# Linear attention: the gate's logits taken through the values, half of the last softmax in the last round, and the end laid out by hand

## Chip, core and metric

The kernel runs on one core of a Trainium2 chip. The metric is the device time of one execution in microseconds; lower is better. The time before is a median of three executions. The profile and its trace come from one more execution of the same kernel.

## The reference

The model is a small vision transformer of two layers over 128 images, 64 tokens for each and 256 features for each token. The part that the change touches is layer 1: a linear attention over normalised features, and the first lines of the mixture of experts behind it, which need the logits of a gate over the sum.

```python
# layer 1: attention, h is [128 images, 64 tokens, 256]; C = 64, H = 8 heads of 32
q, k, v = heads(ln(h) @ Wq.T + bq), heads(ln(h) @ Wk.T + bk), heads(ln(h) @ Wv.T + bv)
q = softmax(q, axis=-1) * sqrt(d)         # over features
k = softmax(k, axis=-2)                   # over positions
context = einsum('bhnd,bhne->bhde', k, v)
out = einsum('bhnd,bhde->hbne', q, context)
h = h + back_to_tokens(out)
# layer 1: experts
x = ln(h)
logits = x @ gate_w + gate_b              # [8192 tokens, 8 experts]
idx = argmax(softmax(logits))             # each token's expert, then gather, two products, scatter
```

The kernel computes the product of k, q and v in the other order: for each half of a group it forms the 64x64 matrix of `scores` between q and k and mixes the values by it.

## The kernel before

The kernel has stages that follow one another: tokenizer, attention with relu, an attention of experts, and then `linear_attention`, `route` and `experts`. Only `linear_attention`, the tables in `Routing` and the first lines of `route` are touched. An image is a partition (128 of them), and h lies in memory as `hd`, `[image, token, feature]`.

`linear_attention` treats the 64 tokens as 16 groups of four (`Group`) and the 256 features as 4 pairs of head halves (`Heads`, n from 0 to 3). A group is loaded (L1131), its statistics are taken on DVE (`statistics`, L1139 and L1140), `factors` on POOL makes the inverse root, `normal` on ACT normalises (L1150), and `transpose` brings it into feature order in `xT` by eight transposes on PE (L1159) and two copies on ACT (L1160).

The work stands in four rounds of 16 steps, one round for each n, in an order written out by hand (`manual_schedule`; an engine's instructions run in that order). Each step i of round n makes the query and key product of one token (`queries_keys`, L1182, four passes of 512 columns), then `prepare` does a piece of a later group: statistics of group g+3, normalisation of group g+1, and at the last of every four steps the transposes of group g+1 and the load of group g+5. Then come the steps listed in `work` for (n, i), then the bias add that takes the product out of PSUM on DVE (`queries_keys_kept`, L1186), and in eight of the steps two tokens' value products (`values`, L1196) with a copy on ACT (L1199). Products of both kinds share three PSUM buffers.

The list `work` is filled by `at(round, step, function)`. For head n it holds, in round n+1:

- `values_transposed` (L1209, eight groups of four transposes, with bias by ACT at L1212).
- `largest`, `maximum`, `spread`, `q_less`: the maximum of q over features, by DVE and two small PE products.
- `k_max` (L1249, DVE), `k_less` (L1253, POOL), `k_exp` and `q_exp` (L1257 and L1243, ACT), `k_sum` (L1260, DVE), `k_over_sum` (L1266, POOL).
- `scores` (L1275, 128 passes, two halves alternating), `scores_kept` and `scores_sums` (`am`, L1281 to L1288).
- `mixed` (L1297, four steps of 32 passes), `added` (L1305, DVE, into h) and `written` (two stores of 2 MB, L1309). h itself is loaded at step 8 of the head's own round (L1174).

In round n+2 the new h of head n is brought into feature order by 32 transposes (`transposed`, L1319, copies on ACT at L1323), multiplied by the gate's weights (`gates`, L1332) and added to `lgs` (L1342 and L1344), and `moments` takes 64 statistics for the later norm (L1313). After the last round there are no more queries, and the rest of heads 2 and 3 runs as rounds 4 and 5 without them. This is the tail. `route` (from L1518) then joins the statistics, turns `lgs` back by eight transposes (L1533), and subtracts the mean's part (L1539).

Of the kernel before, what the change touches and what calls it, by code (L numbers as in the profile page):

```python
# [14 lines left out]
ALU = mybir.AluOpType  # L15
# [1068 lines left out]
def linear_attention(c, hd, hx, out, lgs, sth, wqk, bqk, wv, bv, wgb):  # L1084
# [4 lines left out]
    tc, nc = c.tc, c.nc  # L1089
    NG = 4  # L1090
    with (
# [17 lines left out]
        wgs = wp.tile([P, 4, 32], F32, name="wgs")  # L1109
        nc.gpsimd.memset(wgs, 0.0)  # L1110
        for j in range(2):
            r = slice(j * 64, j * 64 + 64)
            nc.scalar.dma_start(wgs[r, :, j * E : j * E + E], wgb.rearrange("(p f) e -> f p e", f=64))
        ones = wp.tile([P, P], F32, name="ones")
        nc.gpsimd.memset(ones, 1.0)
# [6 lines left out]
        class Group:  # L1122
# [10 lines left out]
            def statistics(self, j):  # L1133
                if j == 0:
                    self.mv = gp.tile([P, NG, 2], F32, tag="mv", name="mv", bufs=4)
                    self.rs = gp.tile([P, NG], F32, tag="rs", name="rs", bufs=4)
                    self.nb = gp.tile([P, NG], F32, tag="nb", name="nb", bufs=4)
                st = gp.tile([P, 6], F32, tag="st", name="st")
                nc.vector.bn_stats(st, self.x[:, j, :])  # L1139
                nc.vector.bn_aggr(self.mv[:, j, :], st)  # L1140

            def factors(self):
                mean, var = self.mv[:, :, 0], self.mv[:, :, 1]
                nc.gpsimd.tensor_scalar_add(self.rs, var, LN_EPS)
                nc.gpsimd.tensor_tensor(self.rs, self.rs, c.nhalf[:, 0:NG], ALU.pow)
                nc.gpsimd.tensor_mul(self.nb, mean, self.rs)
                nc.gpsimd.tensor_sub(self.nb, c.zero[:, 0:NG], self.nb)

# [13 lines left out]
        class Heads:  # L1162
# [9 lines left out]
            def load(self):  # L1172
                self.h = hp.tile([P, T, 64], F32, tag="h", name="h", bufs=2)
# [30 lines left out]
            def values_transposed(self, k):  # L1204
# [3 lines left out]
                for j in range(4):  # L1208
                    nc.tensor.transpose(pt[:, j, :], self.v[:, 4 * k + j, :], c.ident)  # L1209
                for j in range(4):  # L1210
                    d = 4 * k + j
                    nc.scalar.activation(self.vT[:, d, :], pt[:, j, :], AF.Identity, bias=bvs[:, d : d + 1])  # L1212


            def largest(self, n):
# [5 lines left out]
                else:  # L1221
                    for s in (4, 2, 1):
                        nc.vector.tensor_max(self.m[:, 0:s], self.m[:, 0:s], self.m[:, s : 2 * s])

# [38 lines left out]
            def k_over_sum(self, hh, n):  # L1263
                eng = nc.vector if self.n == 3 and hh == 1 else nc.gpsimd
# [5 lines left out]
            def scores(self):  # L1270
                self.pa = pss.tile([P, 64], F32, tag="ps", name="pa")
                for d in range(32):
                    for hh in range(2):
# [41 lines left out]
            def transposed(self, k):  # L1315
                pt = pst.tile([P, 4, B], F32, tag="pt", name="pt")
                for j in range(4):
                    t = 8 * k + 2 * j
                    nc.tensor.transpose(  # L1319
                        pt[:, j, :], self.h[:, t : t + 2, :].rearrange("p t f -> p (t f)"), c.ident  # L1320
                    )
                hT = hp.tile([P, 4, B], F32, tag=f"hT{k % 4}", name="hT")
                nc.scalar.copy(hT, pt)  # L1323
                if k % 4 == 0:
                    self.hT = []
                self.hT.append(hT)

            def gates(self, x):

                self.pg = pso.tile([P, 4, B], F32, tag="po", name="pg")  # L1330
                for s in range(4):
                    nc.tensor.matmul(  # L1332
                        self.pg[s * 32 : s * 32 + 32].rearrange("p j b -> p (j b)"),
                        wgs[:, self.n, :],
                        self.hT[s].rearrange("p j b -> p (j b)"),
                        start=True,
# [550 lines left out]
```

## Time and profile before

| | us |
|---|---|
| median of 3 executions | 2783.39 (2780.57 to 2786.43) |
| the profiled execution | 2789.24 |
| its span | 2787.4 |
| PE busy | 2610.8 (94% of the span) |
| DVE busy | 2042.3 (73%) |
| ACT busy | 1611.1 (58%) |
| POOL busy | 1629.6 (58%) |

Busy time counts from the start of an instruction to its end. Matmuls are pipelined, so the time between two starts is the better price of one. A 32-bit product is two passes, and each is a row's count in the trace. "PEclk" is the clock that was granted to TensorE, as a share of full speed. An arrow behind a row names what ended the idle time ahead of it.

### The profile page before, as it was taken

The page shows a single profiled execution, that of the slowest core. Times are in us where ns is not written, and L with a number is a line of the kernel's source. Part 1 is how long each engine was busy: PE and PEld are TensorE (multiplying, and loading weights), DVE is VectorE, ACT ScalarE, POOL GpSimd, SP SyncE. Part 2 cuts the span into 40 slices and gives each one's busy share as a digit, 9 for nine tenths or more (in the row PEclk, how much of TensorE's full clock was granted, in tenths as well). Part 3 has the DMA queues.
Part 4 walks back from the last instruction along what each step waited for, and adds up shares of the span by engine and source line. Part 5 has one row for each costly group of instructions (what it writes and reads, how often), then busy time and mean ns, then how long its engine had stood idle before and what let it go on. Part 6 is the DMA issues. An engine that isn't in the chain of part 4 may idle for free. (4 is left out here: it accounts for less than half of the span.)

```text
span 2787.4 us, 76931 instructions
## 1 busy us (share of the span) xinstructions
PE 2610.8 (94%) x33260; PEld 1749.5 (63%) x33260; DVE 2042.3 (73%) x3077; ACT 1611.1 (58%) x3347; POOL 1629.6 (58%) x1389
## 2 busy tenths in 40 slices
PE   7989999999999998899999999998899964999997
PEld 3553444444444443688888888887566644888886
DVE  6759999999998997577777877776566766344443
ACT  3228889888888886466665665665344430233332
POOL 3329888888888897765566655643133211454444
PEclk9999999999999999899999999999899975999999
DMA  3000000000000000000000000000444432555554
GB/s 107 31 12 1 2 1 2 1 2 2 1 2 1 2 2 2 12 11 18 11 18 11 11 18 11 18 10 19 113 96 108 101 83 108 169 191 192 195 194 132
DMA packets 138064, 140.81 MB, mean 51 GB/s; under 512 B 107923, under 2 KB 121509, under 8 KB 130032
## 3 DMA queue, kind: packets, MB, share of 16 engines
q1 hardware_dynamic: 126816, 117.91, 14.1%
q0 software_dynamic: 7648, 14.77, 1.7%
q8 instruction: 263, 4.31, 0.6%
q10 hardware_dynamic: 3248, 3.09, 0.4%
q14 instruction: 89, 0.73, 0.1%
HBM read 103.93 MB, written 32.54 MB: 49 GB/s over the span
## 5 line engine op out<-in xcount | busy, mean ns | idle before, releaser
L495 POOL TENSOR_TENSOR m<-q,k 128x1024 f32<-128x1024 f32 x384 | 719.4, 1906 | 30.6 <-PE sc L297 16.3
L487 DVE TENSOR_TENSOR m<-pc,k 128x2048 f32<-128x2048 f32 (+1 forms) x320 | 646.7, 2058 | 0.5 <-ACT q L431 0.5
L297 PE MATMUL sc<-m,wide 128*32 128x512 f32 x4096 | 529.6, 598 | 12.1 <-DVE m L487 7.2
L496 ACT ACTIVATE m<-m 128x1024 f32<-128x1024 f32 x384 | 402.3, 1049 | 6.0 <-POOL m L495 5.4
L297 PEld LDWEIGHTS sc<-m,wide 128*32 128x32 f32 x4096 | 126.5, 109 | 259.8 <-issue 144.6
L505 ACT ACTIVATE m<-k,q 128x64 f32<-128x64 f32 x1024 | 270.9, 339 | 0.8 <-DVE k L378 0.8
L946 DVE TENSOR_REDUCE mx<-sc 128x16 f32<-128x1024 f32 x128 | 156.1, 1219 | 155.2 <-PE sc L934 125.5
L961 POOL TENSOR_TENSOR e<-e,mx 128x1024 f32<-128x1024 f32 x128 | 243.6, 1903 | 10.1 <-POOL mx L960 0.2
L906 ACT COPY qk<-pqk 128x512 f32<-128x512 f32 x256 | 138.8, 603 | 132.6 <-PE pqk L902 132.6
L960 POOL TENSOR_TENSOR mx<-mx,gate 128x16 f32<-128x16 f32 x128 | 27.8, 217 | 315.5 <-ACT z L991 154.5
L1722 PE MATMUL ph<-xt,w1s 128*128 128x256 f32 x896 | 201.1, 383 | 1.2 <-DVE xt L1713 0.8
L1738 PE MATMUL po<-w2s,hT 128*128 128x256 f32 x896 | 198.0, 379 | 0.0
L973 ACT COPY pT<-pt 128x512 f32<-128x512 f32 x256 | 138.7, 598 | 99.4 <-PE pt L970 98.7
L1722 PEld LDWEIGHTS ph<-xt,w1s 128*128 128x128 f32 x896 | 171.8, 192 | 26.1 <-DVE xt L1713 1.2
L1726 ACT ACTIVATE hT<-ph,w1s 128x256 f32<-128x256 f32 x224 | 93.4, 471 | 155.4 <-PE ph L1722 82.9
L1738 PEld LDWEIGHTS po<-w2s,hT 128*128 128x128 f32 x896 | 168.1, 190 | 21.7
L902 PE MATMUL pqk<-xT,w 64*128 64x128 f32 x2048 | 169.3, 289 | 1.9 <-issue 1.9
L947 DVE TENSOR_TENSOR e<-sc,mx 128x1024 f32<-128x1024 f32 x128 | 156.7, 1224 | 4.4
L1756 POOL DMA_INDIRECT out<-y,rout x56 | 56.8, 1014 | 172.6 <-ACT hT L1726 124.9
L953 DVE TENSOR_REDUCE mx<-e 128x16 f32<-128x1024 f32 x128 | 153.2, 1197 | 2.4 <-ACT e L950 2.4
L902 PEld LDWEIGHTS pqk<-xT,w 64*128 64x128 f32 x2048 | 142.5, 189 | 19.5 <-issue 10.9
L970 PE MATMUL pt<-ident,e 128*128 128x128 f32 x1024 | 142.4, 279 | 4.7 <-POOL e L961 1.2
(289 smaller groups left out, 4985.7 us busy)
## 6 DMA issues: line engine op xcount, KB each, us to landing
w1s<-in_we SPq DMA_DIRECT2D x30, 1028.0 KB
w2s<-in_we SPq DMA_DIRECT2D x30, 1024.0 KB
hd<-h SPq DMA_DIRECT2D x16, 512.0 KB
x<-hd SPq DMA_DIRECT2D x16, 512.0 KB
h<-hd SPq DMA_DIRECT2D x4, 2048.0 KB
hx<-h SPq DMA_DIRECT2D x4, 2048.0 KB
out<-h SPq DMA_DIRECT2D x4, 2048.0 KB
xt<-in_x SPq DMA_DIRECT2D x15, 512.0 KB
```

Source lines behind the costliest of these rows:

```text
L297: nc.tensor.matmul(dst[j : j + 32], wide[:, hf, s : s + 32], part, start=start, stop=stop)
L487: nc.vector.tensor_tensor(m, bcast(self.pq[:, hf, i : i + n], 3, T), k, ALU.max)
L495: nc.gpsimd.tensor_tensor(m, bcast(self.q[:, hf, s : s + 2], 3, T), k, ALU.subtract)
L496: nc.scalar.activation(m, m, AF.Relu)
L505: nc.scalar.activation(self.parts[i, hf][:, q], self.blk.k[:, hf, i], AF.Relu, bias=self.q[:, hf, i - NB // 2, q : q + 1], scale=-1.0,)
L902: nc.tensor.matmul(pq[par][:, k, eh, :], w[r, f : f + P], self.xT[r, fc], start=True, stop=True)
L946: nc.vector.tensor_reduce(mx, sc, AX.X, ALU.max)
L947: nc.vector.tensor_sub(e, sc, bcast(mx, 2, T))
L953: nc.vector.tensor_reduce(self.sm[x], self.e[x], AX.X, ALU.add)
L961: nc.gpsimd.tensor_mul(e, e, bcast(sm, 2, T))
L1722: nc.tensor.matmul(ph[:, j], self.w1[:, w0 : w0 + P], self.xt[:, fc], start=(fc == 0), stop=(fc == 1))
L1738: nc.tensor.matmul(po, self.hT[:, f, r * P : r * P + P], self.w2[:, f, :], start=(f == 0), stop=(f == 7))
```

## The change

The gate's logits are no longer made from the new h. They are a sum of two parts, the one from the h before the attention and the one from the attention's output. The first comes from the normalised groups, through a table `wm` that also holds the gate's own weights: `gates` multiplies `xT` by it in four calls in the head's own round, at steps 1, 5, 9 and 15. Eight of the nine parts of the result go into `u`, a set of values that are already multiplied by the gate; the ninth, times the group's deviation `sd`, is added to `lgs`. `u` is transposed in round n+1 (`gates_transposed`) and mixed by the same `am` as the values (`gates_mixed`), and one addition puts the result into `lgs`, which now lies in token order. The table is made at the start, from three new inputs, by 17 products. `route` takes the difference between the new mean and the group's, which is kept in `mvs`.

In the rounds, `largest` and what follows it stand two steps later, the statistics of `moments` move from steps 8 to 11 to the round's end and the next one's first two steps, the load of h moves into round n+1, and h has a single buffer (for head 3, a buffer of the queries and keys). For head 3, the first half of the softmax stands in steps 9 to 15 of the last round. The end is a written list, `last`, with some of the bias adds on DVE in place of ACT.

```diff
-        wgs = wp.tile([P, 4, 32], F32, name="wgs")
...
+        wm = wp.tile([P, 2, 8, 9, E], F32, name="wm")
+        ub = wp.tile([P, 4, E], F32, name="ub")
+        tmp = hp.tile([P, 32 * P], F32, tag="v", name="tmp")
+        nc.sync.dma_start(tmp[0:32, 0 : 8 * D], wvT)
+        nc.sync.dma_start(tmp[0:32, 8 * D : 8 * D + P], bvT)
+        nc.sync.dma_start(tmp[0:32, 9 * D : 9 * D + 64], wgd)
+        wgd = tmp[0:32, 9 * D : 9 * D + 64]
+        for fc in range(2):
+            pw = pst.tile([P, 8, 8, E], F32, tag="pt", name="pw")
+            for g in range(8):
+                o = g * D + fc * P
+                nc.tensor.matmul(pw[:, g].rearrange("p h e -> p (h e)"), tmp[0:32, o : o + P], wgd, start=True, stop=True)
+            nc.vector.tensor_copy(wm[:, fc, :, 0:8].rearrange("p h e g -> p g h e"), pw)
+            nc.vector.tensor_copy(wm[:, fc, :, 8], bcast(k.wgs[:, fc], 1, 8))
...
+                nc.gpsimd.tensor_mul(self.sd, self.sd, self.rs)
...
-                self.h = hp.tile([P, T, 64], F32, tag="h", name="h", bufs=2)
+                if self.n == 3:
+
+                    h = hp.tile([P, 2, 32, P], F32, tag="qk", name="h3", bufs=2)
...
+                else:
+                    self.h = hp.tile([P, T, 64], F32, tag="h", name="h")
...
+            def gates(self, q):
...
+                pu = pso.tile([P, NG, 9, E], F32, tag="po", name="pu")
+                for j in range(NG):
+                    for fc in range(2):
+                        nc.tensor.matmul(
+                            pu[:, j].rearrange("p o e -> p (o e)"),
+                            g.xT[:, fc, j, :],
+                            wm[:, fc, 2 * self.n + q // 2].rearrange("p o e -> p (o e)"),
...
+                nc.scalar.copy(
+                    self.u.rearrange("p e (t g) -> p e t g", g=8)[:, :, q * NG : q * NG + NG],
...
+                nc.vector.tensor_mul(b, pu[:, :, 8], bcast(g.sd, 2, E))
+                nc.vector.tensor_add(o, o, b)
...
+            def gates_mixed(self):
+                self.pg = pss.tile([P, E, T], F32, tag="ps", name="pg")
+                for e in range(E):
+                    nc.tensor.matmul(self.pg[:, e, :], self.uT[:, e, :], self.am, start=True, stop=True)
...
+            def spread_of(self, hh):
+                pool, tag = (pss, "ps") if hh else (pst, "pt")
+                self.pb = pool.tile([P, 64], F32, tag=tag, name="pb")
+                nc.tensor.matmul(self.pb, ones[0:64], self.dg[0:64, 0:64], start=True, stop=True)
...
-                eng = nc.vector if self.n == 3 and hh == 1 else nc.gpsimd
+                eng = nc.vector if (hh, n) == (1, 0) else nc.gpsimd
...
+            if n > 0:
+                y = heads[n - 1]
+                for i in range(4):
+                    at(n + i // 2, (15, 15, 0, 1)[i], y.moments, 16 * i, 16)
+            at(m, 3, x.load)
             for i in range(4):
-                at(m, 3 + i // 2, x.k_less, i // 2, i % 2)
-                at(m, 4 + i // 2, x.q_less, i)
+                at(m, 2 + i // 2, x.largest, i)
+            at(m, 4, x.maximum)
+            at(m, 4, x.k_max, 0)
...
+            at(m, 5, x.k_max, 1)
...
+                at(m, (5, 6, 6, 7)[i], x.q_less, i)
             for hh in range(2):
-                at(m, 5 + hh, x.k_exp, hh)
-                at(m, 6 + hh, x.q_exp, hh)
...
+                at(m, 6 + hh, x.k_exp, hh)
+                at(m, 7 + hh, x.q_exp, hh)
+                at(m, 7 + hh, x.k_sum, hh)
+                at(m, 8 + hh, x.k_over_sum, hh, 1)
+                at(m, 8 + hh, x.k_over_sum, hh, 0)
...
+            for i in range(2):
+                at(m, 8 + i, x.gates_transposed, i)
...
+            at(m, 12, x.gates_mixed)
+            at(m, 13, x.gates_added)
...
+        at(3, 9, x.largest_of, 0)
+        at(3, 11, x.load)
+        at(3, 11, x.maximum_of, 0)
+        at(3, 12, x.spread_of, 0)
+        for i in range(2):
+            at(3, 11, x.k_less, 0, i)
+            at(3, 12 + i, x.q_less_of, 0, i)
...
+        at(3, 14, x.k_sum, 0)
+        for n, x in enumerate(heads):
+            for q in range(4):
+                at(n, (1, 5, 9, 15)[q], x.gates, q)
+
+        def last():
+            x, y = heads[3], heads[2]
+            x.k_max(1)
+            x.values(0)
...
+            x.largest_of(1)
+            x.values(1)
+            x.values(2)
+            x.k_exp_of(1, 0)
+            x.maximum_of(1)
+            x.values(3)
...
+            x.values(6)
+            y.moments(0, 16)
+            x.scores((0,))
+            x.values(7)
+            y.moments(16, 8)
+            x.scores((1,))
+            x.scores_kept()
+            x.gates_transposed(0)
+            x.scores_sums()
+            x.gates_transposed(1)
+            for k_ in range(8):
+                x.values_transposed(k_)
+            x.gates_mixed()
+            x.mixed(0)
+            x.gates_added()
+            y.moments(24, 8)
+            for k_ in range(4):
+                x.added(k_)
+                if k_ < 3:
+                    x.mixed(k_ + 1)
+                    y.moments(32 + 8 * k_, 8)
+            x.written()
+            y.moments(56, 8)
+            x.moments(0, 64)
...
-        pl = gpp.tile([P, 2, 4, 4, 32], F32, name="pl")
...
+        nc.vector.tensor_sub(mean, mean, k.mvs[:, :, 0])
         nc.vector.tensor_mul(dev, bcast(k.wsum, 1, T), bcast(mean, 2, E))
...
+        nc.vector.tensor_sub(pb, k.lgs.rearrange("p e t -> p t e"), dev)
```

## The prediction, made before the changed kernel was run

> **What bounds the kernel now.** First I read the table of busy time by stage, to see where the change lies and which engine fills it. The columns are length, then busy time of PE, PEld, DVE, ACT and POOL, the granted clock, the DMA share and GB/s.
>
> ```profile
> core 0: us, PE busy (x) PEld busy (x) DVE busy (x) ACT busy (x) POOL busy (x), PEclk, DMA share, GB/s
> 1964.00:2012.00 48.00, 47.76 (x163) 28.88 (x162) 20.57 (x50) 16.94 (x33) 7.42 (x19) 0.95 0.42 90
> 2012.00:2079.00 67.00, 62.47 (x454) 42.30 (x454) 43.95 (x78) 32.74 (x69) 21.55 (x24) 1.00 0.30 64
> 2079.00:2155.00 76.00, 71.59 (x503) 47.72 (x502) 53.43 (x144) 37.38 (x77) 21.55 (x24) 0.98 0.52 122
> 2155.00:2217.00 62.00, 56.36 (x430) 34.19 (x429) 44.43 (x115) 29.72 (x63) 16.63 (x12) 0.97 0.42 88
> 2217.00:2290.00 73.00, 57.43 (x461) 43.69 (x460) 47.71 (x165) 28.88 (x60) 11.25 (x6) 0.81 0.41 101
> ```
>
> Rows one to four are rounds 0 to 3 (16 steps each), row five is the tail up to the routing. The rounds are bound by TensorE, so work added there costs its full length; the tail is a chain across engines at a clock of 0.81. What follows the tail (routing, experts) begins when it ends.
>
> Then the chain that starts the first round, from the timeline:
>
> ```profile
> 1958.86 0.25 POOL L1144 TENSOR_SCALAR rs<-mv 128x4 f32<-128x4 f32 x1 [7.87 <-DVE mv L1140]
> 1960.83 2.07 ACT L1150 ACTIVATE x<-x,nb,rs 128x256 f32<-128x256 f32 x4 [17.06 <-DMA x<-hd]
> 1961.48 2.81 PE L1159 MATMUL pt<-ident,x 128*128 128x128 f32 x8 [5.87 <-ACT x L1150]
> ```
>
> It goes from the last statistics on DVE over POOL and ACT to PE; the first query product stands at 1964.11. Next, the waits of PE from 1964 to 2290 (total, times, longest):
>
> ```profile
> PE pt L1159 <- ACT x L1150: 8.6, 3, 4.0
> PE po L1297 <- DVE am L1288: 5.0, 4, 2.3
> PE pq L1182 <- DVE qk L1186: 1.4, 1, 1.4
> ```
>
> The first is the transposes of x at step 7, behind the exponents on ACT. Last, TensorE rows that price what is new:
>
> ```profile
> 1328.26 1.84 PE L854 MATMUL pg<-wrs,xT 128*128 128x4 f32 x16
> 1329.96 1.07 PE L970 MATMUL pt<-ident,e 128*128 128x128 f32 x8
> ...
> 2061.27 2.00 PE L1297 MATMUL po<-am,vT 64*128 64x64 f32 x32
> 2063.20 1.99 PE L1196 MATMUL pv<-wvs,xT 128*128 128x256 f32 x8
> ...
> 2260.69 12.45 PE L1297 MATMUL po<-am,vT 64*128 64x64 f32 x128 [2.31 <-DVE am L1288]
> 2274.51 3.81 PE L1319 MATMUL pt<-ident,h 128*128 128x128 f32 x16 [1.37 <-DVE h L1305]
> 2253.56 3.95 PE L1275 MATMUL pa<-qk 128*64 128x64 f32 x128
> ```
>
> From start to start: 16 passes with 128-column weights and only 4 moving columns take 1.70 us (0.107 each), a `mixed` step 1.93 at full clock; four of them in the tail take over 12.45, since the clock there is 0.50:
>
> ```profile
> 2265.00:2268.00 3.00, 3.00 (x32) 3.00 (x32) 1.28 (x2) 0.00 (x0) 0.00 (x0) 0.50 0.00 0
> 2268.00:2271.00 3.00, 3.00 (x32) 3.00 (x32) 1.25 (x2) 0.00 (x0) 0.00 (x0) 0.50 0.00 0
> ```
>
> **TensorE work per head.** Removed: 8 groups of 4 transposes at 0.435 and two `gates` at 1.77, 7.0 us; it lay two rounds later, so rounds 2 and 3 had it and the tail had two heads of it. Added: four `gates` of 16 passes with 128-column weights and 72 moving columns. A row with 4 columns gives 0.107 a pass, one with 256 columns 0.216; I take 0.107, as the load of the weights covers 72 columns (64 alone run at 0.060). That is 1.71 a call, 6.9 a head, in the head's own round. Bounds: 0.060 (4 us less a head) and 0.107+0.060=0.167 (4 us more). Besides, 8 transposes of `u` (0.87) and `gates_mixed`, 16 passes at 0.107 (1.71), a round later.
>
> **Start.** New on PE ahead of the transposes: 16 small products, 32 passes with 128-column weights, plus 2 for `ub`. PE is at half clock there (four such passes 0.99 us at 1954.62), and 0.107 doubles to 0.213: 7.2 us from about 1955.9, when `tmp` has landed (issued with the rest at 1949.7, as long in flight as x, 6.6 us, or a little less). The order of DVE puts statistics 2 and 3 of group 0 behind the copies of these products: copies end at about 1963.7, statistics at 1964.4 in place of 1958.7. The chain shifts: **+5.7** (+2, were PE at full clock, to +7).
>
> **Round 0.** 44.8 us of dense PE work and a cold start fill it; four `gates`: **+6.9**.
>
> **Rounds 1 and 2.** The first had 61.7 us of PE work and 5.3 of waits (67.0); the second 68.7 and 7.0 (75.75). PE work becomes 61.7+9.4=71.1 in both. Waits: at step 1 DVE now has the product and sum of `gates` (0.42) ahead of the bias add, so it stands until PE has done `gates` (7.2 us into the round) and is free at 8.2. From there it has `largest` (2.4 and 2.6), `maximum` 0.5, `k_max` 2.2 twice, `q_less` 1.12 four times, `k_sum` 2.56 and in each step statistics 0.55 and bias add 0.6, with no gap. Added up, m is ready at 14.9 (PE stands 1.2 for it), the bias adds of steps 5, 6 and 7 end at 24.3, 27.7 and 32.5. As PSUM holds three products, PE waits 1.3, 0.8 and 1.0 for those. With 1.0 for `am`, as before: 5.3 less what starts earlier, 4.9 in all, so 76.0 each. The wait on ACT goes: of the exponents only one `k_exp` (1.9) now stands ahead of the last normalisation of step 7, and DVE is what is late next. **+9.0** and **+0.2**.
>
> **Round 3.** 53.3 us of work and 9.0 of waits before (62.3). Work +2.9 (9.4 and 0.5 of the half softmax, less 7.0): 56.2. DVE gains the half softmax (2.6+2.2+0.5+2.3+2.6=10.2) and loses half the moments (4.1). Waits: 1.2 for m, 1.5 for the normalisation (POOL's two `k_less` of 1.9, then `k_exp`, end at 24.3), 2.3 ahead of the scores for POOL's three `k_over_sum` (1.9 each, from 30.0), 1.0 for `am`. Then DVE waits at step 12 in `q_less_of` for `pb`, which PE makes only after `mixed(1)` and `gates_mixed`; behind it stand the bias add and `added(1)`, which frees PSUM for `mixed(2)`: 2.3 in all. Sum 64.5: **+2.2**.
>
> **Tail.** Before, 73.0 from 2216.8. After, counted from the end of `gates`: `k_max` and `largest_of` on DVE end at 6.1, PE stands 1.0, seven `values` of 1.72 end at 13.4 with the maximum and exponents of half 1 beside them; scores of one half: the two halves run side by side (0.0305 a pass for both, under the 0.053 that 64 columns need at 512 columns in 0.427), so one alone takes 64 passes at about 0.058, 3.7; `values(7)` 1.7; the other half 3.7: 22.5. Ten groups of transposes, each waiting for a copy (0.65 on DVE, 1.1 on ACT) of the buffer two before: 31.5. `gates_mixed` 1.71, doubled at half clock to 3.4, `mixed` 13.65 (four starts 3.41 apart), 48.6. Last `added` 1.4, `moments` 8 and 64 at 0.13: 59.3. **-13.7**. Half clock is the choice here, as the stretch of transposes before it is like that of 2241 to 2250, which lost the clock. At full clock the end is 51.5 (-21.5); with scores at 1.95 each, 3.5 less.
>
> The trace shows continuous PE work at 0.50 from 2262.4 to 2274, in `mixed` alone. "TensorE: Matmul & The Clock Gate" of the Trainium skill (section "What's actually happening") says that a busy window of about 3.4 us returns the full clock; no window does so in that stretch. By the rule the tail would be about 6 us shorter than by the row; I go by the row.
>
> **Moved DMAs and other things at no cost.** The load of h stands three steps into the next round, on SP behind a load of x, and its single buffer waits for the last head's two writes (4.2 MB at 217 GB/s, 19.3 us). It is issued some 13 us into the round, lands 10 us later and is used at 49; x behind it on SP is fetched four groups ahead. If that cover goes, up to 10 us. The write of head 3 starts at 50 of the tail and needs 19.3; the gather from it comes 55 us after. POOL's extra product (0.2, 16 times) and ACT's copies of `u` (0.41, 16 times, against 32 of 0.54 removed) lie beside PE. Routing: 8 transposes and 8 small subtractions were hidden; a subtraction of 128x512 (0.6) and of 128x64 come: **+0.6**, 0 to 0.9.
>
> **Sum.** 5.7+6.9+9.0+0.2+2.2-13.7+0.6=+10.9. The profiled execution took 2789.24 (span 2787.4), 5.9 above the median of 2783.39; it would become 2800.1, the median **2794.3**.
>
> **Rivals.** *Dense rounds* (the other side): the 16 us of waits of rounds 2 and 3 vanish, since ACT no longer delays step 7 and DVE's lag fits into three PSUM buffers. Rounds 1 to 3 are then 71.5, 71.5 and 57, together -5.0 in place of +11.4: total -5.5, median 2777.9; it turns faster by this much once DVE's bias adds of steps 5 to 7 end 3 us sooner than I count. For it: one wait on ACT was 8.6 of PE's. Against: DVE has no slack from step 1 to 8. *Warm tail*: the clock stays at 1.0: 7.8 less than forecast, +3.1, median 2786.5; against it the two rows at 0.50. *Dear gates*: load and product don't overlap, 0.167 a pass: 16 calls by 0.96, +15.4, median 2810; against it 256-column rows that hide the load. *The half softmax isn't done in time*: its last POOL step ends 0.8 us into the tail and is used at 13.4, so this costs nothing; the built order has every step where it is said to be.
>
> **How the numbers follow.** Forecast 0.53, dense rounds 0.15, warm tail 0.17, dear gates 0.10, others 0.05. About 0.2% (5.6 us) is what a measurement can tell from no change. The forecast's own range, from its bounds, is 2787 to 2802; the full one 2777 to 2808. Slower: nearly all of forecast and dear gates, a third of warm tail: 0.68. Faster: half of dense rounds and half of the others, with a share of 0.05 of warm tail in which waits go too: 0.15. The rest, 0.17, is the same.
>
> **What would show it.** Right: first query product about 5.7 us later; round 0 near 55, rounds 1 and 2 near 76, round 3 near 64, tail near 59 with `mixed` at 0.50 and 3.4 apart; L854's 0.107 in `gates`; PE waiting for DVE's bias add, no longer for ACT's normalisation. Wrong: rounds 1 and 2 near 71, or `mixed` 1.93 apart.

## The result, and the profile after

The changed kernel took 2804.89 us (median of 7, 2798.19 to 2812.98), the kernel before 2786.69 in the same sittings (median of 7, 2780.57 to 2792.56): a ratio of 1.0067, 95% interval 1.0049 to 1.0085. It is slower, as forecast, by 18 us where 11 were forecast; 2804.89 lies above the forecast's own range (2787 to 2802) and inside the full one (to 2808). The kernel before was itself 3.3 slower in these sittings than the 2783.39 that the forecast started from.

The profiled execution took 2804.89 (span 2803.2). A table of stages says where the time went. The stage begins with SP's first issue after the last store of hd; a round runs from its first query product to the next round's, round 3 to the first value product behind it (in the changed kernel behind its last `gates`), and the tail from there to the first instruction of the routing on DVE.

| us | before | after | difference | forecast |
|---|---|---|---|---|
| start, to the first query product | 15.27 | 23.28 | +8.0 | +5.7 |
| round 0 | 47.70 | 53.72 | +6.0 | +6.9 |
| round 1 | 66.96 | 76.98 | +10.0 | +9.0 |
| round 2 | 75.75 | 78.53 | +2.8 | +0.2 |
| round 3 | 62.29 | 71.84 | +9.6 | +2.2 |
| tail | 72.98 | 58.93 | -14.1 | -13.7 |
| routing and experts | 497.61 | 498.54 | +0.9 | +0.6 |
| sum | 838.56 | 861.82 | +23.3 | +10.9 |

The spans differ by 15.8 only, since the untouched stages ahead were 7.5 shorter in the second execution (the stage began at 1941.38 in place of 1948.84). That is chance: in twelve more executions with the same code ahead it began anywhere from 1938.6 to 1950.7. The stage table is therefore the better measure of an edit here; a median decides only what is over some 5 us (an estimate, from the intervals in the table of experiments).

The busy time by stage of the changed kernel (length, then PE, PEld, DVE, ACT and POOL, granted clock, DMA share, GB/s), rounds 1 to 3 and the tail:

```profile
2018.38:2095.36 76.98, 72.24 (x542) 52.07 (x541) 52.93 (x120) 36.31 (x80) 21.65 (x27) 1.00 0.27 56
2095.36:2173.89 78.53, 73.92 (x542) 53.10 (x541) 56.70 (x152) 36.25 (x80) 21.66 (x27) 0.98 0.51 116
2173.89:2245.73 71.84, 63.65 (x474) 42.64 (x472) 57.20 (x105) 33.10 (x70) 24.70 (x16) 0.93 0.53 105
2245.73:2304.66 58.93, 40.17 (x383) 34.59 (x382) 44.09 (x165) 11.27 (x21) 7.46 (x3) 0.86 0.41 98
```

Two figures stand out. Round 2 has the work of round 1 and took 1.55 more, at a clock of 0.98. Round 3 has 57.2 us of DVE (44.4 before) and a clock of 0.93. PE's waits from the first query product to the end of the tail (total, times, longest):

```profile
PE pm L1320 <- DVE m L1315: 4.9, 1, 4.9
PE pq L1208 <- ACT v L1225: 3.5, 2, 1.8
...
PE pm L1345 <- DVE m L1301: 2.5, 3, 0.9
PE pv L1222 <- ACT v L1225: 1.9, 2, 0.9
```

The 8.6 for ACT's normalisation are gone, as forecast (1.0 is left). What came is not the bias add on DVE but the copies of the value products on ACT (3.5 and 1.9), and in the tail 4.9 for m. The chain that starts the first round, from the timeline:

```profile
1942.77 0.42 SPq L1117 DMA_DIRECT2D tmp<-in_bvT  x1
1946.21 0.31 SPq L1118 DMA_DIRECT2D tmp<-in_wgd  x1
1946.57 18.66 SPq L1150 DMA_DIRECT2D x<-hd  x5
1950.15 7.05 PE L1124 MATMUL pw<-tmp 32*128 32x64 f32 x32 [2.37 <-DMA tmp<-in_wgd]
1950.97 0.43 DVE L1159 BATCH_NORM_STATS2 st<-x 128x6 f32<-128x256 f32 x1 [2.98 <-DMA x<-hd]
1957.24 1.06 DVE L1125 COPY wm<-pw 128x512 f32<-128x512 f32 x1 [1.45 <-PE pw L1124]
1959.43 0.25 POOL L1164 TENSOR_SCALAR sd<-mvs 128x4 f32<-128x4 f32 x1 [15.82 <-DVE mvs L1160]
1962.04 2.80 PE L1180 MATMUL pt<-ident,x 128*128 128x128 f32 x8 [4.41 <-ACT x L1171]
```

x is there at 1950.97, but the last statistics of its group stand behind the second copy of the table, and POOL starts on them at 1959.43. The table's products take 7.05 (forecast 7.2). Not forecast is SP: after the store of hd and four loads it stood for 3 us (1943.2 to 1946.2) ahead of the table's last load, so x, behind it, was issued 5.2 after the stage's first issue, where before it was 0.9.

In round 3 TensorE's own rows are long:

```profile
2218.56 0.43 PE L1404 MATMUL pr<-am,share 128*128 128x64 f32 x2 [1.28 <-DVE am L1400]
2220.55 3.68 PE L1416 MATMUL po<-am,vT 64*128 64x64 f32 x32 [1.56 <-DVE am L1407]
2224.38 2.94 PE L1208 MATMUL pq<-w,xT 128*128 128x512 f32 x4
...
2236.63 3.68 PE L1208 MATMUL pq<-w,xT 128*128 128x512 f32 x4
...
2285.49 7.36 PE L1416 MATMUL po<-am,vT 64*128 64x64 f32 x128
```

A `mixed` step of 3.6 from start to start (1.93 at full clock) and query products of 2.9 and 3.6 (1.8) are half clock, 4.5 us in all. The last row is the tail's `mixed`: 7.36, full clock, where the forecast had 13.65. And DVE beside POOL at the start of the tail:

```profile
2249.60 0.68 DVE L1311 TENSOR_TENSOR m<-qk 128x512 f32<-128x512 f32 x1
2250.31 4.58 DVE L1313 TENSOR_TENSOR m<-m,qk 128x512 f32<-128x512 f32 x2
...
2249.76 4.59 POOL L1371 TENSOR_TENSOR qk<-qk,ks 128x1024 f32<-128x1024 f32 x2 [5.16 <-DVE ks L1367]
```

The two steps of L1313, which take 1.42 together in round 3 (at 2212.78, when POOL is still), take 4.58 while POOL subtracts. The 3.2 more are most of PE's 4.9.

### The profile page after: what moved, and what is told of

It is laid out like the page before. It is cut to its first block, busy times and chain, and to the rows that moved or that the text cites. A ratio compares the mean times of both kernels' runs of the same rounds, so it can differ in the third digit from the quotient of the medians.

```text
span 2803.2 us, 77355 instructions
## 1 busy us (share of the span) xinstructions
PE 2618.8 (93%) x33449; PEld 1773.5 (63%) x33449; DVE 2065.6 (74%) x3123; ACT 1599.9 (57%) x3335; POOL 1633.5 (58%) x1402
## 3 DMA queue, kind: packets, MB, share of 16 engines
q1 hardware_dynamic: 126960, 118.20, 14.1%
```

## The experiments

Each run is the changed kernel with one edit (e8_tail lays the whole tail out again, e9_full puts parts together), and the table has their stages from one profile each. The ratio is to the kernel before.

| run | start | round 0 | 1 | 2 | 3 | tail | ratio, 95% interval |
|---|---|---|---|---|---|---|---|
| changed kernel | 23.28 | 53.72 | 76.98 | 78.53 | 71.84 | 58.93 | 1.0067 (1.0049 to 1.0085) |
| e1_start | 17.89 | 54.03 | 76.98 | 76.85 | 74.03 | 58.83 | 1.0057 (1.0040 to 1.0074) |
| e2_max_first | 23.32 | 53.78 | 76.98 | 78.52 | 71.86 | 53.67 | 1.0057 (1.0040 to 1.0073) |
| e3_round3 | 23.81 | 54.07 | 76.98 | 76.86 | 69.83 | 59.24 | 1.0085 (1.0056 to 1.0115) |
| e4_half_gates | 23.44 | 50.95 | 77.65 | 78.33 | 71.08 | 59.55 | not comparable |
| e5_act_copies | 23.31 | 54.33 | 76.99 | 76.85 | 70.64 | 60.50 | 1.0072 (1.0047 to 1.0097) |
| e6_values_first | 23.25 | 54.37 | 77.99 | 76.16 | 70.63 | 58.85 | 1.0075 (1.0048 to 1.0103) |
| e7_no_half | 23.75 | 54.29 | 76.99 | 76.85 | 66.5 | 76.7 | 1.0129 (1.0096 to 1.0161) |
| e8_tail | 23.53 | 54.36 | 76.99 | 76.84 | 70.61 | 47.98 | 1.0045 (1.0029 to 1.0061) |
| e9_full | 17.00 | 54.54 | 75.37 | 75.24 | 67.10 | 49.76 | 1.0007 (0.9992 to 1.0022) |
| e10_no_pool | 23.70 | 54.82 | 76.98 | 76.85 | 68.99 | 57.59 | 2797.90 us, one time |
| e11_gap | 23.24 | 53.95 | 76.99 | 76.85 | 70.56 | 57.99 | 2801.57 us, one time |
| e12_late_sums | 24.42 | 54.43 | 76.98 | 76.84 | 70.61 | 68.87 | 2823.44 us, one time |

Where an edit leaves a stage alone, the column shows its spread. Round 2 is 76.85 in eight such runs and 78.5 in two: one stretch at half clock, or none. Round 3 lies between 69.0 and 74.0 with the same instructions, most often near 70.6, so an edit of round 3 shows a gain only when it falls below that spread.

**The start: e1_start.** VectorE does group 0's statistics ahead of the copies of the table.

```diff
-            nc.vector.tensor_copy(wm[:, fc, :, 0:8].rearrange("p h e g -> p g h e"), pw)
...
+            table_products()
             for g in range(3):
                 for i in range(NG):
                     groups[g].statistics(i)
                 groups[g].factors()
                 if g == 0:
+                    table_kept()
+                    table_rest()
...
```

> Only the order at the start differs: VectorE does the statistics of group 0 first and the copies of the table's products behind them; the products stay where they are on TensorE. Theory A (the statistics stood behind the copies): the first query product comes about 19 us after the stage's first issue on SP (23.3 in the changed kernel, 15.3 before); the products end at 15.8, two rows of transposes and a copy follow. Round 0 stays at 53.7. Total -4.5 us, median near 2800.5. Rival B (what is late is the load of x behind the table's, and the products at half clock; the order on VectorE is hidden behind both): the first query product stays at 22 us or more, total within 1.5 us of the changed kernel. Rival C: the copies, now later, hold the two PSUM buffers of the transposes, so the transposes wait for them: 21 us, -2.

The first query product stands at 17.89: 5.4 of the 8.0 were this order. Theory A, and a little more than it said. The other 2.6 over the kernel before are the later load and the table itself: x is used 9.64 after the first issue, before it was 7.62. From the first issue to the routing the run takes 358.6 for the changed kernel's 363.3, rounds 2 and 3 moving by -1.7 and +2.2 beside it.

**DVE beside POOL: e2_max_first and e10_no_pool.** The first puts the queries' maximum ahead of the keys' maximum, behind which POOL starts; the second leaves the order and lets DVE do POOL's subtraction.

```diff
-            x.k_max(1)
+            x.largest_of(1)
             x.values(0)
+            x.k_max(1)
             x.k_less(1, 0)
             x.k_less(1, 1)
-            x.largest_of(1)
```

> In the tail alone the maximum of half 1 over the queries is put ahead of the maximum of the keys, so that GpSimd's subtraction starts only when the maximum is done. Theory A (VectorE's maximum, which reads two tensors in SBUF, stands still while GpSimd works on its own tensor: its two middle steps took 4.58 us in the changed kernel where 1.42 is their length elsewhere): L1313 takes 1.42 again, TensorE's wait of 4.9 for m goes, and with it the stretch at half clock behind it (a value product pair of 3.62 and one start of 2.0 lost): tail 59 becomes 52 to 54, total -5 to -7. Rival B (the steps are slow for a reason of their own, such as the strided half of the tile or the DMA at 217 GB/s beside them): L1313 stays near 4.6, the wait only moves by the 2.2 of the maximum of the keys, which now stands behind: total -2 to -3. Rival C (the exponents of the keys, now later by 3 us, become what the scores wait for): the wait for m goes, a wait of 3 to 5 ahead of the scores comes: total within 2.

```diff
-                nc.gpsimd.tensor_sub(x, x, bcast(self.ks[:, hh, 16 * n : 16 * n + 16], 2, 64))
+                eng = nc.vector if (self.n, hh) == (3, 1) else nc.gpsimd
+                eng.tensor_sub(x, x, bcast(self.ks[:, hh, 16 * n : 16 * n + 16], 2, 64))
```

> In the tail alone the subtraction of the keys' maximum of half 1 is done by VectorE in place of GpSimd, in the same place of the order (ahead of the queries' maximum). Theory A (VectorE's steps with two operands in SBUF stand still while GpSimd works on a tensor of its own): L1313 takes 1.42 for its two steps in place of 4.58, the subtractions 1.2 each on VectorE; m comes 0.5 to 1 us sooner than in the changed kernel although VectorE has 2.4 more to do. Rival B (the order, the strided half of the tile or the DMA beside it makes these steps slow): L1313 stays near 4.6 and m comes 2.4 later.

From the timelines of DVE, first of e2_max_first and then of e10_no_pool:

```profile
2252.96 1.42 DVE L1313 TENSOR_TENSOR m<-m,qk 128x512 f32<-128x512 f32 x2
2257.84 1.80 DVE L1324 TENSOR_SCALAR dg<-ident,mc 64x64 f32<-64x64 f32 x1
```

```profile
2243.95 2.36 DVE L1372 TENSOR_TENSOR qk<-qk,ks 128x1024 f32<-128x1024 f32 x2
2246.95 1.42 DVE L1313 TENSOR_TENSOR m<-m,qk 128x512 f32<-128x512 f32 x2
```

Theory A in both: 1.42 for the two steps when POOL is still or has nothing to do, in the old order too, with the same store of some 217 GB/s beside it. In e10_no_pool m is ready 0.8 sooner after the keys' maximum has begun, with 2.4 more work on DVE. In e2_max_first the next victim is seen: the small product that makes dg (0.25 in the changed kernel) took 1.80, as POOL had begun 0.15 ahead of it, and PE stood 1.9 for it. The tail is 5.3 shorter all the same. Steps that take one operand from PSUM (`q_less`, 1.21 with POOL at work and without) or that reduce one tensor (`k_max`, 2.28 in both cases) are not touched.

"SBUF — State Buffer" of the Trainium skill (section "SBUF: two separate sides") states this: GpSimd and VectorE share one pair of ports by an exclusive lock, held for a whole instruction, and a VectorE step with two SBUF inputs needs it beside a GpSimd step that reads SBUF. These runs agree, 0.69 alone and 2.28 beside POOL. The forecast priced every DVE step by its row alone and missed it.

**Round 3: e3_round3 and e7_no_half.** The first reorders the half softmax; the second takes it out of the round.

```diff
-            if m == 3:
-                at(m, 10, heads[3].k_max, 0)
             at(m, 10, x.scores_kept)
             at(m, 11, x.scores_sums)
+            if m == 3:
+                at(m, 11, heads[3].largest_of, 0)
...
-        at(3, 9, x.largest_of, 0)
+        at(3, 9, x.k_max, 0)
...
```

> In round 3 alone: the keys' maximum of half 0 moves ahead of the scores (step 9), the queries' maximum behind the sums of the scores (step 11), the steps that follow from it go one step later each. Theory A (VectorE came late to am, because its maximum stood still beside GpSimd's normalisation, 2.39 in place of 0.68, and the keys' maximum of 2.27 stood ahead of am; TensorE then lost its full clock): TensorE's waits of 1.3 and 1.6 around the sums of the scores fall to about 0 and 0.9, mixed of step 11 runs in 1.93 in place of 3.61 and query product 12 in 1.8 in place of 2.9; round 3 goes from 71.7 to 66 to 68; total -4 to -6. Rival B (the round is longer by the work of the half softmax itself and by the wait for pb, whatever the order): round 3 stays above 70, the waits only come at steps 12 to 14, total within 2.

```diff
-        at(3, 9, x.largest_of, 0)
...
         def last():
             x, y = heads[3], heads[2]
+            x.k_max(0)
+            x.k_less(0, 0)
...
+            x.k_over_sum(0, 1)
             x.k_max(1)
```

> The half softmax of the last head is taken out of round 3; both halves stand in the tail, the same steps, half 0 first. Theory A (round 3 grew by the half softmax on VectorE, in queue and through the clock): round 3 from 71.8 to 64 to 66, the forecast's 64.5 without the half being 60 to 62; the tail gets 10 to 14 longer, since VectorE's 10 us of half 0 stand ahead of half 1 and TensorE has nothing but values to do; total +3 to +7. Rival B (round 3 is bound by the other heads' chain and by the gates): round 3 stays at 70 or more, total +10 or more. Rival C (eight value products cover the half in the tail): tail +4 or less, total -2 to -4, and the half softmax inside the round is a loss.

In e3_round3 all that theory A names came true: DVE's first step of the maximum 0.68 in place of 2.39, no wait ahead of the sums, 0.91 ahead of `mixed`, which ran in 1.93, and query product 12 after it at full clock. Yet the round is 69.8, 2.0 less than in the changed kernel's profile and 0.8 less than the usual 70.6: inside the spread of round 3, so no gain is shown. The timeline of PE, and the clock at the scores, show where the rest went:

```profile
2207.73 0.33 PE L1394 MATMUL pa<-qk 128*64 128x64 f32 x2 [1.38 <-POOL qk L1384]
2208.90 5.46 PE L1394 MATMUL pa<-qk 128*64 128x64 f32 x126 [0.85 <-DVE qk L1384]
...
2236.80 3.52 PE L1208 MATMUL pq<-w,xT 128*128 128x512 f32 x4
```

```profile
2210.00:2213.00 3.00, 3.00 (x62) 3.00 (x60) 2.41 (x3) 0.00 (x0) 0.54 (x2) 0.50 0.01 3
2213.00:2216.00 3.00, 3.00 (x45) 2.05 (x43) 1.60 (x4) 0.00 (x0) 3.00 (x2) 0.97 0.04 9
```

The waits of 1.38 and 0.85 ahead of the scores, which were there in the changed kernel too, are now followed by half clock in the scores (5.46 for 3.9), and query product 14 is slow as before. A wait of about 1 us costs the clock in some executions and not in others. So neither theory as it stood: the queue was right, and half clock elsewhere gave the gain back.

e7_no_half goes the other way by much. Counted to the end of `gates`, round 3 is 66.5, so the half softmax costs 4.1 there (against 70.6). The tail becomes 76.7: PE stands 10.0 and 8.9 for the two maxima, each slowed by POOL again. The half in the round thus saves some 13 net. No theory had the size: the round came nearest to A, the total to B.

**Rounds 1 and 2: e4_half_gates and e6_values_first.** The first leaves out half of the gates' products (the second half of the features), the second moves value products.

```diff
-                    for fc in range(2):
+                    for fc in (0,):
                         nc.tensor.matmul(
...
```

> The gate products use only the first of the two feature chunks (8 passes a call in place of 16), so the logits are not those of the reference; all copies, sums and later steps stay. Theory A (TensorE bounds the rounds, each pass costs 0.107 on the path): each of the 16 calls is 0.86 us shorter, rounds 0 to 3 are 3.4 shorter each: total -13.7. Rival B (VectorE and ScalarE set rounds 1 to 3, as their waits show): only round 0 shortens by 3.4, rounds 1 to 3 by 1 or less as the waits grow: total -4 to -6. Rival C (the weight load and the product do not overlap, 0.167 a pass): total -21.

```diff
+                    early = n in (1, 2) and i in (6, 7, 8)
+                    if early:
+                        x.values(i - 6)
                     for step in work.pop((n, i), ()):
                         step()
...
```

> In rounds 1 and 2 the value products of steps 6, 7 and 8, and with them their copies on ScalarE, stand ahead of the exponents of these steps; nothing else moves. Theory A (the value copy behind an exponent that waits for GpSimd holds the PSUM buffer of the next query product): the waits of 1.8 and 0.9 on ScalarE's value copies go in both rounds, round 1 from 77.0 to 74 to 75, round 2 from 78.5 to 74 to 76, total -4 to -6. Rival B (the exponents then come later by the copies, and the scores wait for the keys' normalisation on GpSimd in their place): rounds stay within 1 of 77.0 and 78.5 with a new wait of 1 to 3 ahead of the scores. Rival C (VectorE's bias adds of steps 5 to 7, late behind the maxima, are what PSUM waits for, as the forecast had it): the waits move to the bias add with 0.8 to 1.3 each, rounds shorten by 1 or less.

e4_half_gates takes some 0.9 off each call (1.74 became 0.85). Round 0 gets 2.8 shorter, rounds 1 to 3 do not: theory B. (Its experts get other tokens, so its total says nothing.) From its waits of PE in round 1, and its clock just behind the first:

```profile
PE pq L1208 <- ACT v L1225: 2.7, 1, 2.7
PE pm L1345 <- DVE m L1301: 1.6, 1, 1.6
```

```profile
2044.00:2048.00 4.00, 2.06 (x3) 1.03 (x4) 3.93 (x8) 2.38 (x3) 3.18 (x2) 0.66 0.01 2
2048.00:2052.00 4.00, 4.00 (x13) 2.73 (x12) 3.97 (x6) 1.13 (x3) 1.76 (x5) 0.50 0.02 4
```

A third of the 3.4 that PE saves in round 1 turns into longer waits for the same chain of DVE, POOL and ACT (1.8 became 2.7, 0.9 became 1.6, another 0.9 became 0.5), and the half clock behind the longest, of some 5 us, takes the rest. Rounds 1 to 3 are thus not bound by PE alone: the chain ends close behind it.

In e6_values_first the waits on the value copies fall from 1.8 and 0.9 to 0.7 and none, a wait of 0.6 for the bias add comes, and round 2 is 0.7 shorter than 76.85. Round 1 is 1.0 longer, by a stretch at half clock (one row of value products, 3.64 in place of 1.99). Part of A and part of C: the exponents were ahead of the copies, but DVE stands close behind them.

**The tail: e5_act_copies, e8_tail, e11_gap and e12_late_sums.** In e5_act_copies ScalarE makes all copies of the last head's transposes.

```diff
-                if self.n == 3 and k % 3 < 2:
+                if False:
...
-                if self.n == 3:
+                if False:
```

> In the tail alone, ScalarE makes all copies of the transposed values and gate products of the last head, as before the change (VectorE makes 8 of the 10 groups in the changed kernel). Theory A (the stretch of transposes decides the clock of what follows): the stretch from the first transpose of u to gates_mixed goes from 8.1 to about 11.5 (10 groups of 1.14 on ScalarE through two buffers), TensorE stands 0.7 of every 1.14, loses its full clock, and gates_mixed and mixed run at 0.50: 3.4 and 13.6 in place of 1.8 and 7.4. Tail 58.9 becomes 68 to 70, total +9 to +11. Rival B (gaps under 1 us do not cost the clock): only the stretch grows, tail 62 to 63, total +3 to +4. Rival C (the copies are hidden, the last statistics on VectorE set the end): VectorE is freed of 5.4 us, tail within 1.

The stretch has gaps of 0.7 at most, and the clock stayed: 1.90 and 7.36 for `gates_mixed` and `mixed`. The tail is 1.6 longer, less than rival B's 3 to 4, as the stretch of transposes grew by 1.5 only. Theory A fell.

```diff
-            for k_ in range(8):
+            for k_ in range(6):
+                x.values_transposed(k_)
+            y.moments(24, 24)
+            for k_ in range(6, 8):
                 x.values_transposed(k_)
...
-            y.moments(24, 8)
...
```

> In the tail alone 24 of head 2's statistics on VectorE (3.1 us) stand ahead of the copies of the last two groups of transposed values, so that TensorE waits 2 to 3 us just before gates_mixed and mixed; the work is the same. Theory A (one such gap costs the full clock, and light passes of 64 columns do not bring it back, as in the tail before): gates_mixed and all of mixed run at 0.50, 3.4 and 13.6 us in place of 1.8 and 7.4; tail 59 becomes 66 to 69. Rival B (half clock lasts a fixed time of about 3.4 us after a gap, costing 1.7, whatever runs): mixed takes 8 to 9.5, tail 60 to 63. Rival C (a gap of this length costs no clock): only the gap itself, tail 58 to 61 with mixed at 7.4.

Inconclusive on the clock: no gap came. `gates_mixed` and the first steps of `mixed` do not need the last two groups, so PE went on. (The tail lost 0.9, as fewer statistics stand between the adds behind `mixed`.) So the gap was put where PE has nothing else:

```diff
             x.gates_transposed(0)
-            x.scores_sums()
             x.gates_transposed(1)
             for k_ in range(8):
                 x.values_transposed(k_)
+            y.moments(24, 12)
+            x.scores_sums()
             x.gates_mixed()
...
```

> In the tail alone the sums of the scores (product, reciprocal, product) stand behind the transposes of the values, with 12 of head 2's statistics (1.6 us) on VectorE ahead of the reciprocal, so that TensorE stands 2 to 3 us directly ahead of gates_mixed and mixed, as it stood 2.31 ahead of mixed in the tail before; the same work. (The run with 24 statistics between the copies made no such gap.) Theory A (a gap ahead of light passes costs the clock for as long as they last): gates_mixed and mixed of the changed kernel's 1.8 and 7.4 become up to 3.4 and 13.6; tail 59 becomes 66 to 70. Rival B (half clock is an episode of fixed length, about 3.4 us, that comes a few us behind a gap and costs 1.7): mixed 8 to 9.5, tail 60 to 63. Rival C (the clock stays): mixed 7.4, tail 59 to 61, the gap alone.

```profile
2294.82 3.67 PE L1287 MATMUL pg<-am,uT 128*128 128x64 f32 x16 [2.85 <-DVE am L1407]
2298.43 13.92 PE L1416 MATMUL po<-am,vT 64*128 64x64 f32 x128
```

```profile
2294.00:2298.00 4.00, 3.17 (x15) 3.18 (x16) 0.74 (x3) 0.00 (x0) 0.00 (x0) 0.50 0.00 0
...
2306.00:2312.00 6.00, 6.00 (x60) 6.00 (x58) 3.66 (x16) 0.00 (x0) 0.00 (x0) 0.50 0.00 0
```

Theory A to the number: a gap of 2.85 doubles `gates_mixed` and `mixed` behind it, 3.67 and 13.92, and 17 us without a break do not bring the clock back. The tail is 68.9, 10 longer for a gap of 2.85. The rule weighed in the prediction ("TensorE: Matmul & The Clock Gate" of the Trainium skill, section "What's actually happening", a busy window of about 3.4 us) does not hold for these light passes in this run either. In rounds 2 and 3, where products of 256 and 512 columns run as well, half clock did end, mostly after 3.4 or 6.8 us. But that is no rule that the runs bear out: in round 3 of e1_start it lasted 17 us with two query products in it, and in e3_round3 (above) the scores, light passes of 64 columns too, had the full clock back within their own row. From e1_start:

```profile
2214.00:2228.00 14.00, 14.00 (x59) 9.56 (x58) 4.93 (x9) 1.06 (x1) 0.00 (x0) 0.50 0.36 57
```

```diff
+            x.largest_of(1)
+            for j in range(3):
+                x.values(j)
+            x.maximum_of(1)
             x.k_max(1)
...
-            x.scores((0,))
             x.values(7)
-            y.moments(16, 8)
-            x.scores((1,))
+            x.q_exp_of(1, 1)
+            x.values_transposed(0)
+            x.values_transposed(1)
+            x.scores()
+            y.moments(12, 16)
...
```

> The tail of the changed kernel laid out again, the same work: the queries' maximum of half 1 first and its spread ahead of the keys' maximum, the transposes of u between the value products, the scores of both halves side by side again (64 steps of two at 0.031 each, 3.9, in place of twice 3.9), all statistics of head 2 into VectorE's free stretches so that only head 3's 64 stand at the end. Theory A (the tail is TensorE's work and two waits): TensorE's wait of 4.9 for m goes, the scores take 3.9 less, the last statistics begin 1 us after the last add: tail 58.9 becomes 49 to 52, total -7 to -10. Rival B (the chain keys' maximum, GpSimd, exponents, sums, GpSimd sets the start of the scores): the wait comes back ahead of the scores, 3 us or more, tail 53 to 55, total -4 to -6. Rival C (with the wait goes the clock: transposes ahead of the scores leave TensorE idle and mixed falls to 0.50): tail 56 to 58.

The tail falls to 47.98, below theory A's 49 to 52, with all its parts: no wait for m, scores of both halves in 3.9 together, `mixed` at full clock, only 64 statistics at the end (8.20 in one row).

**All together: e9_full.** The start of e1_start with x loaded earlier, the tail of e8_tail, the order of round 3 with one step more between the scores and `mixed`, and value products ahead of the exponents and between the sums and `mixed`.

> All the lessons in one kernel, the same computation: at the start x before the last of the table's loads, the load of the router's bias behind them, and VectorE's statistics ahead of the copies; in rounds 1 and 2 the values' transposes ahead of the maximum, the value products of steps 6 to 8 and 11 ahead of the exponents and of mixed; in round 3 scores, sums and mixed one step later with query product 11 in the gap, the queries' maximum away from GpSimd's work, the spread ahead of mixed; the tail laid out again. Theory A (the parts add up): first query product at 16 to 18 us after the stage's first issue, round 0 at 54, rounds 1 and 2 at 75 to 76, round 3 at 66 to 68, tail at 47 to 49; 335 to 340 from the first issue to the routing, where before had 341 and the changed kernel 363: ratio to before 0.997 to 1.000. Rival B (clock and queue: each wait that goes moves the episode at half clock, 1.7 each, elsewhere): 341 to 347, ratio 1.000 to 1.003. Rival C (the half softmax, now a step later, is late in the tail): a new wait ahead of the tail's maximum or scores, tail 51 or more, ratio 1.002 or more.

Theory A by the sum of the stages: 339.0 from the first issue to the routing, where the kernel before has 341.0 and the changed one 363.3. The tail (49.76) misses A's 47 to 49: a new wait of 1.9 for DVE stands ahead of the last `gates` of round 3, and the first value products of the tail run at half clock behind it (7.65 in place of some 5.2), which is B's mechanism in one place. The ratio of 1.0007 (0.9992 to 1.0022) is no difference that can be measured from the kernel before, and its interval reaches into both theories. So laid out with care the change costs nothing that can be measured, but what it takes from the tail it gives to the rounds. Whether the kernel before would gain by the same care, no run tells.

## Why the prediction was right, and where it was not

**The sum, the sign and the rivals.** The sum was +10.9, the stages of the two profiles give +23.3 and the medians +18.2; the time fell into the full range all the same, but not by anything that the prediction names for times above 2802: *dear gates*, its one rival on the slow side, did not come. That part is luck. The sign was right: slower, by the gates' passes in rounds 0 and 1 and the longer start against a shorter tail. *Dense rounds* did not come: waits in rounds 1 and 2 sum to 4.7 and 4.6 (forecast 4.9). *Dear gates* did not: 16 passes start to start took 1.74, 0.109 a pass. *Warm tail* came for the clock of `mixed`, but did not make the tail as short as it said. *The half softmax in time* held; POOL's last step ended 1.1 ahead of the tail.

**Start, +8.0 for +5.7.** The step held (statistics behind the copies: 5.4 by e1_start). Mis-sized was the load: the table, "issued with the rest", had its last part behind a pause of 3 us on SP, so its products began 8.8 after the stage's first issue where the sum had 7.1. The trace of before shows such a pause on ACT's queue (3.3 ahead of its fifth load), and it was not read there.

**Rounds 0 and 1, +6.0 and +10.0 for +6.9 and +9.0.** The sums hold. The name of the wait was wrong in rounds 1 and 2: not the bias add but the value copy behind an exponent that waits for POOL. The wait for m was right (0.9 for 1.2).

**Round 2, +2.8 for +0.2.** The forecast's 76.0 stands against 76.85 in eight runs. The rest is a stretch at half clock, 1.7, for which the sum had no term.

**Round 3, +9.6 for +2.2, the step that failed.** Its waits sum to 8.2 (forecast 8.3), and its work, counted by the distances of starts, to 56.1 (forecast 56.2). Missing are 4.5 of half clock behind these waits, and 3.0 that the counting from start to start leaves out, some 1.4 of it in the ends of the ten rows that a wait follows (each runs 0.1 to 0.2 beyond where the next would have started); the rest is not placed. The same slip is in what the sum took from before: its "9.0 of waits" in that round are 5.7 of waits by PE's waits from 2155 to 2217, and the other 3.3 are row ends and a stretch at half clock (3.4 us long, 1.7 lost) behind the wait of 4.0. Round 2's 7.0 are 4.4 of waits in the same way, so the 16 us of waits that *dense rounds* took away were some 10. The waits also have other places than forecast: `am`, for which DVE came late through the lock and the keys' maximum, took 2.8 for 1.0. How much half clock a round gets is in part chance: round 3 was 69.0 to 74.0 in nine executions.

**Tail, 58.93 for 59.3: right by two errors.** The half clock in `gates_mixed` and `mixed`, 7.8 of the sum, did not come. The forecast likened the transposes to those before, but the gaps there were 2.2 and 3.2 us and here 0.6 at most. That DVE and ACT share the copies is not the reason, for in e5_act_copies ACT makes them alone and the gaps are 0.7; before, exponents of 2.0 stood between ACT's copies. Nor did those transposes cost the old `mixed` its clock, for it was back at 2252 and lost again only behind the 2.31 just ahead of `mixed`. From before:

```profile
2244.15 2.02 ACT L1257 ACTIVATE qk<-qk 128x2048 f32<-128x2048 f32 x1
2247.25 1.12 PE L1209 MATMUL pt<-ident,v 128*128 128x128 f32 x4 [3.15 <-ACT vT L1212]
```

```profile
2253.00:2256.00 3.00, 3.00 (x89) 2.84 (x88) 3.00 (x21) 2.18 (x8) 0.00 (x0) 1.00 0.02 5
```

In its place PE stood 3.9 longer for m than forecast, 3.2 of it by the lock, the values behind that wait ran at half clock for some 2 us more, and DVE ended 1.1 later. e12_late_sums shows that the price was right and only its condition wrong; e2_max_first and e8_tail show what the tail is without the other error.

## What to carry to other kernels

When a step is moved to another engine's neighbourhood, look at what GpSimd does at that moment: a VectorE step with two SBUF operands waits for GpSimd's instruction (2.28 for 0.69 here), and the wait shows as a long row, not as idle time. Count a gap of 2 us or more in TensorE's work twice, once for itself and once for the clock behind it: from round 1 on, every gap of 2.2 us or more in these traces came with half clock, at the latest 1.7 us behind its end. Do not put passes like those of `mixed` behind such a gap (13.92 for 7.36). And where two chains end within a microsecond, taking work from one gains little; read first what the other waits for.

## What was not expected of the hardware

The passes of `mixed` (64 moving columns) keep the full clock if they have it, 7.36 for 128 of them, and did not regain it, 13.92 for the same after a gap of 2.85; the scores, 64 columns too, did regain it. In the records of the granted clock half clock comes in whole pieces of 3.41 us: one in round 2, two (6.83) or one in round 3 and the tail, five (17.07) in round 3 of e1_start. One piece costs dense work 1.7 and comes or not with the same instructions: round 2 was 76.85 eight times and 78.5 twice. SP stood for 3.0 to 4.0 us after the store of hd and four loads in the changed kernel and in every run of it, whatever the fifth was; why, no run tells.
